# A selective-scan kernel: products with C of a turn as one GpSimd instruction, and the steps around them put into other turns

## The chip, the cores and the metric

The kernel runs on one core of a Trainium2 chip. The metric is the device time of one execution in microseconds (us). Five engines work side by side, each through its own queue in program order: PE (TensorE, matmuls), DVE (VectorE), ACT (ScalarE), POOL (GpSimd) and SP, which issues the DMAs here. An instruction starts when its engine is free and the semaphores that it waits for have been raised.

## The reference, cut to what matters

Eight images of 48x48 positions and 96 channels pass through four layers, each as `x = x + layer(group_norm(x))`. Layers 0 and 3 (called ss2d) and layer 2 (called `lines`) are selective scans; layer 1 is a spectral layer that the change does not touch. A scan layer does this for four directions over the image (rows, columns, and both backwards), with 192 inner channels d and 16 states s:

```python
xz = x @ in_w;  xc, z = split(xz)
u  = silu(conv(xc) + conv_b)            # 3x3 depthwise in ss2d, 4 taps along the line in `lines`
dt_low, B, C = split(u @ x_proj)        # 6 + 16 + 16 values at each position
dt = softplus(dt_low @ dt_w + dt_b)     # step size, one for each d and position
for each position l in order:           # for each d and each state s
    h = exp(dt[l] * A) * h + dt[l] * u[l] * B[l]
    y[l] = sum over s of h * C[l]
y  = y + D * u                          # then, over the directions, merged
```

In ss2d the merged result is normalised over d, multiplied by `silu(z)` and projected to 96 channels. In `lines` the state starts from zero in every line of 48, each direction is multiplied by `silu(z)` and projected, and added to x.

## The kernel before, in words

**Tiling.** A scan layer is a list of blocks: image ("job") by direction by row group of 10, 10, 10, 10 and 8 lines (480 or 384 columns): 160 blocks a layer. A block has 8 *slots* (two halves of 96 channels by four groups of states), a slot has 3 *units*, and a unit is a tile of 128 partitions by n columns (32 channels by 4 states; a few columns more in ss2d for the carried state). Two slots make a *turn*, so a block has four turns, q0 to q3, a layer 640 turns, the kernel 1920. The number of a slot over all blocks is t or `at`; slot 0 is the first of q0.

**A turn.** For turn t the following are written out, in this order (lines 382 to 403):

- DVE: `scan(t, 0)`, the products dbu = dt·u·B of the next turn's first slot, `scan(t, 1)`, those of the next turn's second slot, `scan(t, 2)`. One scan covers two units and runs in place over dbu (L296).
- ACT: the decay factors exp(dt·A), two units at a time into one of two PSUM buffers `ps_da` (`make_da`, L288), and a copy of B into the PSUM buffer `ps_b` (`copy_b`, L245), from which DVE reads it.
- POOL: the product h·C of the turn before's second slot (`make_hc(t-1, 1)`, L302), the units of dbu that DVE leaves over (`make_dbu`, L264), a preparation of the carried state (`begin`), and the product h·C of this turn's first slot. The table `ON_POOL` says how many of a slot's three units POOL makes: slots 1, 3 and 7 two, slot 5 three.
- PE: `reduce(t-1, 0)` and `reduce(t-1, 1)`, each 4 x 3 = 12 matmuls in tiles of the array (L322) and 4 more (L324), which sum h·C over states. They wait for the products.

**Beside the scans.** Twice in a turn `aside` is called, after `reduce(t-1, 1)` for the slot `at = 2t` and at the turn's end for `at + 1`. It loads B and C of the next block (`load_bc`) and its step sizes (`load_dd`) in the slots that `LOAD_BC` and `LOAD_DD` name, takes one step of the side work (`next(beside)`), runs the planned steps of slot `at`, and then what `later` and `tail` hold. All of these stand in the engines' queues at that place.

- The planned steps are `stage1` of a block to come: the projection to dt_low, B and C (ss2d: s0, L642; copied to `bcl` by ACT, L647), the step sizes (`raw`, L632; `biased`, L636; softplus, L660), their products with u on POOL (`make_du`, L449, one instruction for each half, two in a block), and the stores to DRAM (`store_dd`, L434), from which `load_dd` broadcasts them. `plan` places them two blocks ahead, at slots 0 to NG+2 with NG = 8. In `lines` the steps are the convolution (L771), its silu (L778), the projection (L788), the softplus (L806), the z gate (L812, L820) and the stores.
- The side work of ss2d for job j is `post` of job j-1 (norm and output projection, lines 527 to 586; its steps alternate PE, DVE and ACT and are a slot apart), the group norm of the next job, and from 10 x 8 = 80 used slots on the convolution of the next job (lines 500 to 525): eight slots for each half of a row group, with PE matmuls in six of them, a z matmul in the seventh, and two silu on ACT in the eighth. For the last job `post` runs two steps a slot, behind the row groups as they finish.
- In `lines` the end of a direction's block comes through `done`: DVE's product with the gate (L834), one slot later `project` on PE (L843), another slot later `add` on DVE (L849 or L851).

Softplus, silu and exp lie in different table sets of ACT; a change loads a table.

The buffers of B and C are six tiles (`NBUF`), the first `LEAD` columns of each zero; a tile holds B and then C of one group of states and serves two slots of a block.

Of the kernel before, what the change touches and what calls it, by code (L numbers as in the profile page):

```python
# [31 lines left out]
LOAD_BC = (2, 3, 6, 7)  # L32
LOAD_DD = (4, 5)
NBUF = 6
UP = 96
# [5 lines left out]
CH = 96  # L41
ON_POOL = {1: 2, 3: 2, 5: 3, 7: 2}

# [52 lines left out]
def vss_stack_kernel(ctx: ExitStack, tc: tile.TileContext, i: dict, out: bass.AP):  # L96
# [88 lines left out]

    def scans(dirs, order, restart, a, pools, ps, stage1, opening, done, side, tail):

# [16 lines left out]
        rooms = [pools["dbu"].tile([P, 6 * WMAX], F32, tag="dbu", name="dbu") for _ in range(NG // 2)]  # L204
        bufs = [pools["bc"].tile([P, LEAD + 2 * BMAX], F32, tag=f"bc{n}", name=f"bc{n}") for n in range(NBUF)]
        for buf in bufs:
            nc.gpsimd.memset(buf[:, :LEAD], 0.0)
        for room in rooms:
            nc.gpsimd.memset(room, 0.0)
        dbus, das, bps, bcs, ys = {}, {}, {}, {}, {}  # L210
        later, ends = {}, []
# [8 lines left out]
        def load_bc(t):  # L220

            b, slot = blocks[t // NG], t % NG
            sg = ORDER[slot][1]
            other = t - slot + NG - 1 - slot
            n = min(free, key=lambda n: free[n])
            free[n] = other
            r = bufs[n]
            rows4 = b.bcd[8 * sg:8 * sg + 8, :].rearrange("(s w) n -> s (w n)", w=2)
            nc.sync.dma_start(r[:, LEAD:LEAD + 2 * b.n], rows4.unsqueeze(0).to_broadcast([32, 4, 2 * b.n]))

            lo, hi = LEAD - b.at.start, LEAD + b.n
            bcs[t] = bcs[other] = r[:, lo:hi + b.at.start], r[:, hi:hi + b.n]

        def copy_b(t):

            if t >= NG * len(blocks):
                return
            b, slot = blocks[t // NG], t % NG
            if slot == NG // 2:
                bps[t] = bps[t - 1]  # L240
                return
            if ON_POOL.get(slot) == 3:
                return
            bps[t] = ps("b", 1)
            nc.scalar.copy(bps[t][:, :bcs[t][0].shape[1]], bcs[t][0])  # L245

        def units(tile, b, lo, hi):
            return tile[:, lo * b.m:hi * b.m].rearrange("p (u m) -> p u m", m=b.m)

        def make_dbu(t, engine):  # L250

            if t >= NG * len(blocks):
                return
            b, slot = blocks[t // NG], t % NG
            if t // 2 not in dbus:
                dbus[t // 2] = rooms[t // 2 % (NG // 2)]
            cut = 3 - ON_POOL.get(slot, 0)
            lo, hi = (0, cut) if engine is nc.vector else (cut, 3)
            if lo == hi:
                return  # L260
            o = units(dbus[t // 2], b, 3 * (slot % 2) + lo, 3 * (slot % 2) + hi)[:, :, b.by]
            du = b.got[ORDER[slot][0]][:, lo:hi, 1, b.by]
            by = (bps[t] if engine is nc.vector else bcs[t][0])[:, b.by]
            engine.tensor_mul(o, du, by.unsqueeze(1).to_broadcast([P, hi - lo, by.shape[1]]))  # L264
# [32 lines left out]

        def make_hc(t, sub):
            b, q = turns[t]
            n = b.n  # L300
            h = units(dbus[t], b, 3 * sub, 3 * sub + 3)[:, :, b.at]
            nc.gpsimd.tensor_mul(h, h, bcs.pop(2 * t + sub)[1].unsqueeze(1).to_broadcast([P, 3, n]))  # L302

# [37 lines left out]

        for n, b in enumerate(blocks[:2]):
            plan(b, NG * (n - 2))
        for t in range(-2 * NG, 0):
            run(t)
# [29 lines left out]
        for t, (b, q) in enumerate(turns):  # L375
            at, nblk = 2 * t, t // (NG // 2)
            if q == 0:
                if nblk + 2 < len(blocks):
                    plan(blocks[nblk + 2], at)
                if b.k == order[0] and b.first:  # L380
                    beside = side(b.job)
            scan(t, 0)
            if t > 0:
                make_hc(t - 1, 1)
            make_dbu(at + 2, nc.vector)
            make_da(t, 1)
            make_dbu(at + 3, nc.gpsimd)
            if t > 0:
# [8 lines left out]
            begin(t + 2)  # L397
            make_hc(t, 0)
            make_da(t + 1, 0)
# [4 lines left out]
            if q == NG // 2 - 1 and b.k == order[-1] and b.last:  # L404
                for _ in beside:
                    while tail:
                        tail.pop(0)()
        make_hc(nt - 1, 1)
        for sub in range(2):
# [33 lines left out]

    def make_du(b, half, u):


        n = b.n
        dt, du = sizes(b, half)
        nc.gpsimd.tensor_mul(rows(du, n), rows(dt, n), u)  # L449
        if b.m == b.n:  # L450
            at = SEG - 1 if b.rev else 0
            nc.gpsimd.memset(rows(dt, n)[:, :, at:at + 1], FAR)
        elif half == 0:

# [5 lines left out]
    def ss2d(l, xin, xout, b0=0):  # L460
# [3 lines left out]
        def pool(name, bufs, **kw):  # L464
            return stack.enter_context(tc.tile_pool(name=name, bufs=bufs, **kw))
        wt, big, zp, lnp, xio = pool("wt", 1), pool("big", 3), pool("z", 1), pool("ln", 2), pool("xio", 2)
        zdr = pool("zdr", 3, space=DRAM)
# [31 lines left out]

        def conv(b, blks):  # L500
            if blks[0] == BLKS[0]:
                us[b] = big.tile([DH, 2, L], F32, tag="big", name="u")
                zs[b] = zdr.tile([DH, 2, L], F32, tag="z", name="zd")
            for r0, nr in blks:
                n = nr * SEG
                for half in range(2):
                    pu = side_psum()
                    for slot in range(7):
# [6 lines left out]
                        if slot == 6:  # L515
                            pz = ps("s1", 1)
                            nc.tensor.matmul(pz[:DH, :n], lhsT=w[f"{l}_in"][:, (2 + half) * DH:(3 + half) * DH],
                                             rhs=xpad[:C, 1 + r0:1 + r0 + nr, 1:1 + W], start=True, stop=True)
                        yield
                    s = slice(r0 * W, r0 * W + n)  # L520
                    nc.scalar.activation(us[b][:, half, s], pu[:DH, :n], AF.Silu, bias=w[f"{l}_cb"][:, half:half + 1])
                    z = zp.tile([DH, BMAX], F32, tag="z", name="z")
                    nc.scalar.activation(z[:, :n], pz[:DH, :n], AF.Silu)
                    yield
# [63 lines left out]
        def side(job):  # L588
# [17 lines left out]
            if more:  # L606
                for _ in front(job + 1):
                    used += 1
                    yield
                while used < 10 * NG:  # L610
                    used += 1
                    yield
                yield from conv(job + 1, BLKS)
            else:
# [10 lines left out]
        def stage1(b):  # L625
# [35 lines left out]

            def du(half):
                return lambda: make_du(b, half, u[:, half])

            def store(half):
                return lambda: store_dd(b, half)

            return {0: s0, 1: s1, 3: s3, 4: s4, 5: lambda: biased(1), 6: s6, 7: du(0), 8: du(1),
                    NG + 1: store(0), NG + 2: store(1)}

# [14 lines left out]

        dirs = DIRS_SS
        load_x(0)
        for _ in front(0):
            pass
        for _ in conv(0, BLKS[:3]):  # L690
            pass
        scans(dirs, (0, 1, 3, 2), False, a, pools, ps, stage1, opening, done, side, [])
        for _ in post(nb - 1, BLKS[:1]):
# [4 lines left out]
    def lines(xin, xout):  # L698
# [56 lines left out]
        def stage1(b):  # L755
# [53 lines left out]
            def s7():  # L809
                for half in range(2):  # L810
                    got["z", half] = ps("s1", 2)
                    nc.tensor.matmul(got["z", half][:DH, :n], lhsT=w["l2_inz"][:, b.k, half * DH:(half + 1) * DH],  # L812
                                     rhs=shifted(0)[:C], start=True, stop=True)
                for half in range(2):
                    make_du(b, half, rows(b.ub[:, half], n))

            def s8():
                b.zb = up.tile([DH, 2, BMAX], F32, tag="zb", name="zb")
                for half in range(2):
# [49 lines left out]
        for _ in front(0):  # L869
            pass  # L870
        scans(dirs, range(NK), True, a, pools, ps, stage1, opening, done, side, tail)
        stack.close()
# [288 lines left out]
```

## Time and profile before

| | us |
|---|---|
| median of 3 runs | 18841.26 (18840.8 to 18842.25) |
| profiled execution | 18848.6, span 18846.8, mean granted TensorE clock 0.767 |
| layer 0 (ss2d) | about 119 to 5733 |
| layer 1 (spectral) | about 5800 to 7100 |
| layer 2 (`lines`) | about 7167 to 13077 |
| layer 3 (ss2d) | about 13204 to 18817 |

A block of ss2d takes 35.0 us on average, one of `lines` 37.0. The costliest instructions are the scans (L296, 5760 of them, 2.1 us each), the products with C (L302, 3840, 2.6 us each), the decay factors (L288, 11520, 0.65 us each) and the reductions.

A row of the group view reads: line, engine, operation, output<-inputs, shape and count, then busy time and mean ns of one, then the engine's idle time just before these instructions and what ended it. A row of the timeline reads: start, duration, engine, line, operation, and in brackets the idle time before it with its releaser. Runs of equal neighbours are one row there with a count. "PEld" is TensorE's weight load. A wait for several semaphores is put down to the one that came last.

### The profile page before, as it was taken

The page shows a single profiled execution, that of the slowest core. Times are in us where ns is not written, and L with a number is a line of the kernel's source. Part 1 is how long each engine was busy: PE and PEld are TensorE (multiplying, and loading weights), DVE is VectorE, ACT ScalarE, POOL GpSimd, SP SyncE. Part 2 cuts the span into 40 slices and gives each one's busy share as a digit, 9 for nine tenths or more (in the row PEclk, how much of TensorE's full clock was granted, in tenths as well). Part 3 has the DMA queues.
Part 4 walks back from the last instruction along what each step waited for, and adds up shares of the span by engine and source line. Part 5 has one row for each costly group of instructions (what it writes and reads, how often), then busy time and mean ns, then how long its engine had stood idle before and what let it go on. Part 6 is the DMA issues. An engine that isn't in the chain of part 4 may idle for free.

```text
span 18846.8 us, 169421 instructions
## 1 busy us (share of the span) xinstructions
PE 14864.5 (79%) x53500; PEld 4298.7 (23%) x53500; DVE 16139.5 (86%) x10809; ACT 13830.0 (73%) x20502; POOL 15203.6 (81%) x8316
## 2 busy tenths in 40 slices
PE   6777777777777897888988988888677777777776
PEld 1211211211214562222222222222121121121121
DVE  7999999999993227999999999997999999999998
ACT  6777777777772227888888888886778778778776
POOL 7899899899891007888888888886899999999998
PEclk7776776776767787888888888888777777677776
DMA  4545445445453334444444444443454554554444
GB/s 138 167 166 166 167 166 168 165 166 170 161 171 60 48 46 141 154 146 153 156 147 150 151 155 148 148 154 119 164 170 162 169 170 161 169 168 161 169 166 146
DMA packets 768461, 2836.57 MB, mean 151 GB/s; under 512 B 235724, under 2 KB 298668, under 8 KB 640926
## 3 DMA queue, kind: packets, MB, share of 16 engines
q1 hardware_dynamic: 767558, 2825.75, 45.5%
q8 instruction: 418, 6.85, 0.2%
q14 instruction: 485, 3.97, 0.1%
HBM read 2377.32 MB, written 448.17 MB: 150 GB/s over the span
## 4 chain that ended last, share of the span: by engine, by line
DVE 24%; PE 21%; ACT 18%; POOL 17%; issue 12%; DMA 7%; SPq 0%; POOLq 0%; DVEq 0%; ACTq 0%
DVE dbu L296 15%; POOL dbu L302 12%; DVE dbu L264 7%; ACT ps_da L288 5%; PE ps_s L771 4%; ACT L288 4%; POOL dbu L264 4%; DMA dd<-dd 3%; PE ps_y L322 3%; DMA dd<-dds 2%; PE ps_h L1001 2%; PE ps_y L1014 2%; POOL dds L449 1%; PE ps_side L512 1%; PE ps_s L642 1%
## 5 line engine op out<-in xcount | busy, mean ns | idle before, releaser
L296 DVE TENSOR_TENSOR_SCAN dbu<-ps_da,dbu 128x968 f32<-128x968 f32 (+3 forms) x5760 | 11853.6, 2076 | 1080.1 <-ACT ps_da L288 1002.8
L302 POOL TENSOR_TENSOR dbu<-dbu,bc 128x1440 f32<-128x1440 f32 (+1 forms) x3840 | 10060.1, 2634 | 1877.1 <-DVE dbu L296 1715.4
L288 ACT ACTIVATE ps_da<-dd,w_l_a 128x484 f32<-128x484 f32 (+3 forms) x11520 | 7440.1, 650 | 2865.8 <-DVE dbu L296 2652.9
L322 PE MATMUL ps_y<-dbu,w_red 128*32 128x480 f32 (+1 forms) x23040 | 4834.2, 736 | 2581.2 <-POOL dbu L302 2578.1
L324 PE MATMUL ps_y<-dbu,w_red 128*32 128x480 f32 (+1 forms) x7680 | 4795.5, 736 | 0.0
L264 DVE TENSOR_TENSOR dbu<-dd,ps_b 128x1443 f32<-128x1443 f32 (+7 forms) x3360 | 3895.9, 1159 | 292.9 <-ACT ps_b L245 217.5
L264 POOL TENSOR_TENSOR dbu<-dd,bc 128x962 f32<-128x962 f32 (+7 forms) x1920 | 3889.3, 2026 | 96.5 <-DMA dd<-dd 50.0
L322 PEld LDWEIGHTS ps_y<-dbu,w_red 128*32 128x32 f32 x23040 | 756.2, 125 | 6399.6 <-POOL dbu L302 4693.7
L771 PE MATMUL ps_s<-xpad,w_l_cw 128*128 128x480 f32 (+1 forms) x2560 | 1753.3, 837 | 2.6 <-ACT xpad L144 1.6
L245 ACT COPY ps_b<-bc 128x482 f32<-128x482 f32 (+3 forms) x2880 | 1543.4, 536 | 283.4 <-DVE dbu L264 257.3
L512 PE MATMUL ps_side<-xpad,w_l_cw 128*128 128x480 f32 (+1 forms) x2880 | 1613.8, 688 | 5.8 <-ACT xpad L144 4.5
L288 ACT ACT_TABLE_LOAD x986 | 1265.0, 1283 | 17.3
L133 POOL MEMSET w_l_cw<- 128x1760 f32 (+1 forms) x3 | 5.8, 1942 | 1344.4 <-DVE x L981 1339.0
L642 PE MATMUL ps_s<-u,w_l_xp 96*38 96x480 f32 (+1 forms) x1280 | 932.9, 868 | 2.8 <-ACT dds L636 1.5
L632 PE MATMUL ps_s<-bcl,dtw 6*96 6x480 f32 (+1 forms) x1280 | 830.1, 735 | 125.2 <-ACT dds L636 114.9
L449 POOL TENSOR_TENSOR dds<-dds,u 96x480 f32<-96x480 f32 (+1 forms) x640 | 765.8, 1196 | 182.9 <-ACT dds L660 182.8
L318 PE MATMUL ps_y<-ysum,w_ident 96*96 96x480 f32 (+1 forms) x960 | 754.3, 875 | 134.1 <-ACT ysum L683 133.2
L512 PEld LDWEIGHTS ps_side<-xpad,w_l_cw 128*128 128x128 f32 x2880 | 571.2, 223 | 1119.3 <-issue 922.3
L771 PEld LDWEIGHTS ps_s<-xpad,w_l_cw 128*128 128x128 f32 x2560 | 517.5, 207 | 1075.5 <-issue 976.0
L324 PEld LDWEIGHTS ps_y<-dbu,w_red 128*32 128x32 f32 x7680 | 693.7, 125 | 0.0
L788 PE MATMUL ps_s<-ub,w_l_xp 96*38 96x480 f32 (+1 forms) x640 | 376.8, 724 | 271.9 <-ACT ub L778 271.8
L812 PE MATMUL ps_s<-xpad,w_l_inz 96*96 96x480 f32 (+1 forms) x640 | 506.7, 926 | 79.7 <-ACT dds L806 60.2
(147 smaller groups left out, 11761.0 us busy)
## 6 DMA issues: line engine op xcount, KB each, us to landing
dd<-dd SPq DMA_DIRECT2D x512, 1452.0 KB
bc<-bcd SPq DMA_DIRECT2D x1536, 480.0 KB
dd<-dd SPq DMA_DIRECT2D x256, 1440.0 KB
dd<-dds SPq DMA_DIRECT2D x512, 363.0 KB
dd<-dd SPq DMA_DIRECT2D x128, 1164.0 KB
bc<-bcd SPq DMA_DIRECT2D x384, 384.0 KB
dd<-dds SPq DMA_DIRECT2D x256, 360.0 KB
dd<-dd SPq DMA_DIRECT2D x64, 1152.0 KB
```

What stands on the lines that cost most here:

```text
L245: nc.scalar.copy(bps[t][:, :bcs[t][0].shape[1]], bcs[t][0])
L264: engine.tensor_mul(o, du, by.unsqueeze(1).to_broadcast([P, hi - lo, by.shape[1]]))
L288: nc.scalar.activation(da[:, at:at + b.m], b.got[half][:, u % 3, 0, :], AF.Exp, scale=a[:, b.k, ci:ci + 1])
L296: nc.vector.tensor_tensor_scan(db, da, db, 0.0, ALU.mult, ALU.add)
L302: nc.gpsimd.tensor_mul(h, h, bcs.pop(2 * t + sub)[1].unsqueeze(1).to_broadcast([P, 3, n]))
L322: nc.tensor.matmul(y[32 * g:32 * g + 32, :n], lhsT=wc["red"][:, :32], rhs=hc[:, g, b.at], start=False, stop=(slot == 3))
L324: nc.tensor.matmul(y[DH:, :n], lhsT=wc["red"][:, 32:], rhs=hc[:, 2, b.at], start=(slot == 0), stop=(slot == 3))
L449: nc.gpsimd.tensor_mul(rows(du, n), rows(dt, n), u)
L512: nc.tensor.matmul(pu[:, :n], lhsT=flat[:, at:at + P], rhs=xpad[:, r0 + dy:r0 + dy + nr, dx:dx + W], start=(tap == 0), stop=(tap == 8))
L632: nc.tensor.matmul(got["p"][:DH, :n], lhsT=dtw[2 * NS:, b.k, half, :], rhs=b.bcl[2 * NS:, :n], start=True, stop=True)
L642: nc.tensor.matmul(got["p"][:NBC, :n], lhsT=w[f"{l}_xp"][:, b.k, half, :], rhs=u[:, half], start=(half == 0), stop=(half == 1))
L771: nc.tensor.matmul(got["u", half][:, :n], lhsT=flat[:, at:at + P], rhs=shifted(off), start=(tap == 0), stop=(tap == 3))
```

## The change

1. `make_hc(t)` multiplies all six units of a turn with C in one GpSimd instruction; it is issued after `scan(t+1, 0)`, for the turn that has just ended. So that C of two slots is one operand, the buffers of B and C become one tile with seven places, and the operand steps from one place to the other (backwards where needed).
2. `ON_POOL` becomes two tables, and POOL may make units of a turn's first slot too. ss2d: one unit of slots 2, 5 and 6, three of slots 3 and 7. `lines`: two of slot 3, three of slots 5 and 7, one of slot 6. Both still give nine units a block to POOL. Slot 4 takes over slot 3's copy of B only if there is one.
3. `make_du` multiplies both halves in one instruction; in ss2d it stands at slot 7 only (before at 7 and 8), and the stores at NG and NG+1 (before one later each).
4. In ss2d the projection s0 is at slot -1 (before 0), so blocks are planned three ahead. `load_dd` of the first half is at slot 3 (before 4), in all scan layers.
5. The convolution of the side work starts five slots sooner (after 75 used slots), which puts its silu into another turn; its z matmul goes into `tail`, behind the other steps of its slot.
6. Buffers: the block input in `post` has one instead of two, the gate `zb` in `lines` two instead of three.

The core of the diff:

```diff
-LOAD_DD = (4, 5)
-NBUF = 6
+LOAD_DD = (3, 5)
+NBUF = 7
-ON_POOL = {1: 2, 3: 2, 5: 3, 7: 2}
+ON_POOL_SS = {2: 1, 3: 3, 5: 1, 6: 1, 7: 3}
+ON_POOL_L2 = {3: 2, 5: 3, 6: 1, 7: 3}
...
-        bufs = [pools["bc"].tile([P, LEAD + 2 * BMAX], F32, tag=f"bc{n}", name=f"bc{n}") for n in range(NBUF)]
+        bufs = pools["bc"].tile([P, NBUF, 2 * LEAD + 2 * BMAX], F32, tag="bc", name="bc")
...
-        def make_hc(t, sub):
+        def make_hc(t):
             b, q = turns[t]
             n = b.n
-            h = units(dbus[t], b, 3 * sub, 3 * sub + 3)[:, :, b.at]
-            nc.gpsimd.tensor_mul(h, h, bcs.pop(2 * t + sub)[1].unsqueeze(1).to_broadcast([P, 3, n]))
+            h = dbus[t][:, :6 * b.m].rearrange("p (k u m) -> p k u m", k=2, m=b.m)[:, :, :, b.at]
+            at, to = cs.pop(2 * t), cs.pop(2 * t + 1)
+            bcs.pop(2 * t), bcs.pop(2 * t + 1)
+            end = to + (1 if to > at else -1)
+            c = bufs[:, at:(None if end < 0 else end):to - at, LEAD + n:LEAD + 2 * n]
+            nc.gpsimd.tensor_mul(h, h, c.unsqueeze(2).to_broadcast([P, 2, 3, n]))
...
             scan(t, 0)
             if t > 0:
-                make_hc(t - 1, 1)
+                make_hc(t - 1)
             make_dbu(at + 2, nc.vector)
             make_da(t, 1)
+            make_dbu(at + 2, nc.gpsimd)
             make_dbu(at + 3, nc.gpsimd)
...
             begin(t + 2)
-            make_hc(t, 0)
             make_da(t + 1, 0)
...
-    def make_du(b, half, u):
+    def make_du(b, u):
-        n = b.n
-        dt, du = sizes(b, half)
-        nc.gpsimd.tensor_mul(rows(du, n), rows(dt, n), u)
+        dt, du = [b.dds[:, :, n, b.at].rearrange("p h (r s) -> p h r s", s=SEG) for n in range(2)]
+        nc.gpsimd.tensor_mul(du, dt, u)
...
-                while used < 10 * NG:
+                while used < 10 * NG - 5:
                     used += 1
                     yield
-                yield from conv(job + 1, BLKS)
+                yield from conv(job + 1, BLKS, tail.append)
...
-            return {0: s0, 1: s1, 3: s3, 4: s4, 5: lambda: biased(1), 6: s6, 7: du(0), 8: du(1),
-                    NG + 1: store(0), NG + 2: store(1)}
+            return {-1: s0, 1: s1, 3: s3, 4: s4, 5: lambda: biased(1), 6: s6, 7: du,
+                    NG: store(0), NG + 1: store(1)}
```

## The prediction

> **What bounds the kernel now.** I read the page's busy table first. Its columns are busy time, share of the span and instructions.
>
> ```profile
> PE 14864.5 (79%) x53500; PEld 4298.7 (23%) x53500; DVE 16139.5 (86%) x10809; ACT 13830.0 (73%) x20502; POOL 15203.6 (81%) x8316
> DVE  7999999999993227999999999997999999999998
> PEclk7776776776767787888888888888777777677776
> ```
>
> VectorE leads in the three scan layers (slices of nines); the gap in the middle is the spectral layer, which the change does not touch. GpSimd's 81% and TensorE's 79% are near enough to become the bound locally. Then the costliest groups, for who waits on whom:
>
> ```profile
> L296 DVE TENSOR_TENSOR_SCAN dbu<-ps_da,dbu 128x968 f32<-128x968 f32 (+3 forms) x5760 | 11853.6, 2076 | 1080.1 <-ACT ps_da L288 1002.8
> L302 POOL TENSOR_TENSOR dbu<-dbu,bc 128x1440 f32<-128x1440 f32 (+1 forms) x3840 | 10060.1, 2634 | 1877.1 <-DVE dbu L296 1715.4
> L322 PEld LDWEIGHTS ps_y<-dbu,w_red 128*32 128x32 f32 x23040 | 756.2, 125 | 6399.6 <-POOL dbu L302 4693.7
> ```
>
> VectorE stands idle 1080 us ahead of its scans, 1003 of them for ScalarE's decay factors (ps_da): that is all a better order could win. GpSimd's products with C wait for the scan and TensorE waits for the products (4694 us), so GpSimd is not a bound by itself, but its product starts everything that TensorE does in a turn. The same group from 1000 to 5000 us (an ss2d layer; blocks of 35.0 us, 114 of them) and from 8000 to 12000 us (`lines`; 37.0 us, 108):
>
> ```profile
> L296 DVE TENSOR_TENSOR_SCAN dbu<-ps_da,dbu 128x968 f32<-128x968 f32 (+1 forms) x1368 | 2811.9, 2080 | 262.0 <-ACT ps_da L288 235.6 <-POOL dds L449 15.4 <-POOL dbu L302 6.6
> ```
> ```profile
> L296 DVE TENSOR_TENSOR_SCAN dbu<-ps_da,dbu 128x960 f32<-128x960 f32 (+1 forms) x1297 | 2672.2, 2067 | 252.3 <-ACT ps_da L288 252.0
> ```
>
> So 235.6/114 = 2.1 us a block in ss2d, 2.3 in `lines`. ScalarE's timeline in a convolution block names the causes: softplus and silu with their table loads of 1.28 us, between decay factors.
>
> ```profile
> 1406.78 1.28 ACT L660 ACT_TABLE_LOAD   x1
> 1408.07 1.01 ACT L660 ACTIVATE dds<-dds 96x960 f32<-96x960 f32 x1
> 1409.10 1.28 ACT L288 ACT_TABLE_LOAD   x1
> 1412.26 1.28 ACT L521 ACT_TABLE_LOAD   x1
> ```
>
> Last, a turn with post work, over all engines (start, duration):
>
> ```profile
> 2996.75 2.74 POOL L302 TENSOR_TENSOR dbu<-dbu,bc 128x1440 f32<-128x1440 f32 x1
> ...
> 2999.54 1.02 PE L322 MATMUL ps_y<-dbu,w_red 128*32 128x480 f32 x3 [2.06 <-POOL dbu L302]
> ...
> 3001.30 3.36 PE L548 MATMUL ps_side<-ones,sq 96*96 96x1 f32 x20
> ...
> 3002.64 2.16 DVE L296 TENSOR_TENSOR_SCAN dbu<-ps_da,dbu 128x968 f32<-128x968 f32 x1
> ...
> 3004.73 0.13 DVE L551 COPY var<-ps_side 96x5 f32<-96x5 f32 x1
> ```
>
> The product ends at 2999.5, the reductions follow, then the variance matmuls, and VectorE's copy of their result starts at 3004.73, as they end (3004.66) and as the last scan ends (3004.80). The slack of this handoff from TensorE to VectorE is zero. That place decides my forecast.
>
> **The change, part by part.**
>
> The merged product. L302 costs 2736 ns at 1440 elements and 2227 at 1152 (rows of the ss2d layer): 1.77 ns an element and 0.19 us an instruction. One of 2880 is 0.19+2880×1.77 = 5.29 us against 5.47 for two: 0.19×1920 turns = 357 us of GpSimd. It is not on the path, so I count nothing for it. The operand with C is now strided over the seven buffers. The nearest row for a strided operand is L449, 1.03 us in rows and 1.45 in column views, so 2.63 ns an element, 7.8 us a product; the other end is 5.1, with no fixed cost left. I take 5.3, as the inner rows of C stay contiguous, unlike the column views.
>
> What moves with it: before, slot 0's product ran inside the turn and only slot 1's (2.74) came after the turn's last scan. Now both come after it, and both reductions (four groups of four; starts 0.43 us apart at full clock, at 9028.94 us, and 0.80 at half, at 2999.54) wait for it. TensorE's side work in a turn starts 5.3−2.7 = 2.6 us later, plus 0.8 to 1.6 for the reductions that could be done early before. Behind the waiting matmul in TensorE's queue stand the side matmuls; for them wait VectorE (post, add), ScalarE (raw, silu), and GpSimd (du).
>
> Units of B by turn. On VectorE L264 costs 1632 ns for three units, 630 for one, so about 1130 for two. Per ss2d block before 4×1632+3×630 = 8418, after 3×1632+3×1130 = 8286; `lines` after 4×1632+630+1130 = 8288. That is −0.13 us × 480 = −62 us, contained in the sums below. GpSimd's nine units a block stay (1.05, 1.89 and 2.74 us for one to three). The turn with slots 2 and 3 gets 5.3+1.05+2.74 = 9.1 us of GpSimd in about 9. `lines` loses one copy of B (0.55 us, ScalarE, hidden). Turns change length: VectorE's turn q3 gets 1.05 longer, q0 and q2 shorter.
>
> Step products as one: 1.03×2 against about 1.9 (L575, 960 elements, 1.88). It runs behind softplus and ahead of the next product in GpSimd's queue; the store of half 0 then waits 1 us more. SP's queue is passed by: a load at slot 3 ahead of that store, so later loads of B and C start 4 to 5 us later, needed more than a turn after; counted at 0. The single buffer of the block input makes a load wait for the store before it, four slots (17 us) ahead of its use: 0 too. The z gate's matmul goes behind the other steps of its slot, ahead of its silu still: 0. If these covers are gone, the dearest row is 0.35 us a block (37.3 us of DMA waits in 108 blocks of `lines`), 170 us.
>
> Projection a slot sooner, silu of the convolution in turn q1 instead of q3's end. Of ss2d's 35.7-us convolution blocks 32.8 are VectorE's work, 2.9 stalls. After: 32.7 work; ScalarE in q1 has six decay factors 4.0, copies 1.1, silu with tables 3.8 = 8.9 against a turn of 8.8, so 0.6 to 0.8 late in q2; the chain in q2's end, product 5.3, reductions 1.6, two taps 1.85, raw 1.05, biased 0.65, decay pair 1.37 = 11.8 against 10.9, 0.4 to 1.0 at full clock and 2.0 to 2.6 at half; softplus ahead of the next q0, 1.2. Sum 35.0 to 35.4, or 36.7 to 37.1: −0.7 to +1.4. I take +0.3, as the granted clock lies between (0.71 by the window below): ×140 blocks = **+42 us**.
>
> Post blocks. Ten handoffs of a job (14 jobs) lie within one turn. TensorE is 3.4 to 4.2 us later, VectorE 1.05 earlier in q0 and q2 and later in q1 and q3, and of that part was slack: about 1.2 us stall at full clock, 4.3 at half. 140 handoffs give 168 to 602 us, midway 385; while VectorE waits there, ScalarE gets ahead, which saves up to 2.1 us in each of 88 blocks, 185. That leaves 200; I take 2.5 us a block, 220, with +50 and +600 as ends: **+220 us**.
>
> The clock in question (columns: length, busy time and count of PE, PEld, DVE, ACT, POOL, then granted clock, DMA share, GB/s):
>
> ```profile
> 2996.00:3005.00 9.00, 6.94 (x37) 3.68 (x30) 8.86 (x7) 6.51 (x11) 8.94 (x8) 0.50 0.36 90
> 3011.00:3018.00 7.00, 5.45 (x30) 1.12 (x22) 6.70 (x5) 4.14 (x7) 6.57 (x3) 0.99 0.80 297
> 3000.00:4000.00 1000.00, 760.59 (x2736) 194.91 (x2728) 933.15 (x615) 762.16 (x1150) 911.05 (x513) 0.71 0.50 166
> ```
>
> A reduction takes double in the first stretch. [...]
>
> Other ss2d blocks (320−140−88 = 92) lose a third of their 2.1-us stalls, as softplus now falls into the 9.3-us turn: −0.7×92 = **−65 us**. The last job's post, two steps a slot: **+30**.
>
> `lines`. At q0 the silu stall is 1.57 us a block; the longer q3 takes away 1.4 of it. In q1 the add waits for TensorE:
>
> ```profile
> 9025.00 1.03 POOL L449 TENSOR_TENSOR dds<-dds,ub 96x480 f32<-96x480 f32 x1
> ...
> 9026.16 2.73 POOL L302 TENSOR_TENSOR dbu<-dbu,bc 128x1440 f32<-128x1440 f32 x1
> ...
> 9030.52 1.85 PE L843 MATMUL ps_s<-gated,wo 96*96 96x480 f32 x4 [0.57 <-ACT zb L820]
> ...
> 9032.77 0.62 DVE L851 TENSOR_TENSOR x<-x,ps_s 96x480 f32<-96x480 f32 x1
> ```
>
> The product there ends 2.6 us later, then both reductions (1.6, or 3.2) and L843: 0.9 us of stall at full clock, 2.4 to 4 at half. Row blocks −0.7 to +1.2, taken +0.6×80 = **+48**; column blocks, whose TensorE is idle only 2 to 4 us a block, 0 to +2.3, taken +1.0×80 = **+80**.
>
> Sum: 42+220−65+30+48+80 = +355 us. The profiled execution took 18848.6 us (span 18846.8), 0.04% above the median of 18841.3, so 19,204; I say **19,200**.
>
> **The rivals.**
> 1. Faster, by the stalls. If TensorE's results still come before VectorE asks, the handoffs cost nothing, and silu and softplus, now in turns apart and longer, no longer delay decay factors: half of 1002.8 goes. 18848.6−501 = 18,350. For it: ScalarE's decay factors (L288) wait 2653 us for scans, so it has room; against it: the zero slack at 3004.73. It decides if a handoff stalls under 0.3 us. With TensorE at full clock throughout, in between (handoffs at 0, convolution −0.7×140, others −65, rows −0.7×80): 18,630.
> 2. No change: handoffs cost 220 and the other blocks give it back; 18,840.
> 3. The strided product is dear. GpSimd has 3×1.05+2×2.74+2 = 10.6 us beside four products in 35, so from 6.1 us a product it is the bound; at 7.8 a block takes 42 us: 480×7 = +3400, 22,200. Against it: contiguous inner rows.
>
> **How the numbers follow.** Forecast 0.58, rival 1 0.32 (0.20 at 18,350, 0.12 at 18,630), rival 2 0.06, rival 3 0.04. Upper ends of all terms: 1.4×140+600−0+60+1.2×80+2.3×80 = +1136, which needs all at once; I stop at 19,720 (+870). Low end 18,330, just under rival 1. The forecast's own range is 18,900 to 19,720. A change of 0.2% is about what can be told from none: faster 0.32, same 0.06, slower 0.62.
>
> **What would show it.** Right: products with C near 5.3 us, 1920 of them; idle of L540, L551, L584, L851 for PE in the hundreds of us; clock below 0.767. Wrong: those idle times stay near what they are and idle ahead of L296 for ps_da falls towards 500 us (rival 1); L302 above 6 us and VectorE under 80% busy (rival 3). What would make me wrong most likely is the lateness of TensorE, worked out for one turn and applied to 140 handoffs.

## The result, and the profile after

The changed kernel takes 19,786.9 us (median of 4 runs, 19,766.7 to 19,802.7) against 18,841.8 in the same comparison: 1.0500 times as long, with a 95% interval of 1.0482 to 1.0519. It is 945 us slower. The forecast was slower by 355 us, with 19,720 as the upper end; the direction was right, the size was not, and the time lies outside the range. The profiled execution took 19,766.7 us (span 19,765.0), 918 us of span more than before.

The same lines of the page and the same groups as before, now of the changed kernel. Its line numbers are other: L298 is the scan, L309 the merged product, L329 the reduction.

```profile
PE 14657.8 (74%) x53500; PEld 4423.6 (22%) x53500; DVE 16207.1 (82%) x10329; ACT 13682.4 (69%) x20342; POOL 14882.1 (75%) x6061
DVE  6889889888883227888888888886888888888888
PEclk7777777777767778888888888887777777777776
...
L298 DVE TENSOR_TENSOR_SCAN dbu<-ps_da,dbu 128x968 f32<-128x968 f32 (+3 forms) x5760 | 11823.6, 2075 | 1286.5 <-ACT ps_da L290 1099.0
L309 POOL TENSOR_TENSOR dbu<-dbu,bc 128x2880 f32<-128x2880 f32 (+1 forms) x1920 | 9760.3, 5083 | 2067.3 <-DVE dbu L298 1978.5
...
L329 PEld LDWEIGHTS ps_y<-dbu,w_red 128*32 128x32 f32 x23040 | 973.1, 139 | 8037.0 <-POOL dbu L309 5904.6
```

GpSimd is busy 321 us less (357 were worked out for the product), and every other engine is busy for a smaller share. No engine became the bound; all wait more for each other. TensorE's weight loads wait 5905 us for the product (4694 before). VectorE's waits of the changed kernel (line that waits, for whom: us in total, times, longest) show where the time arrived:

```profile
DVE dbu L298 <- ACT ps_da L290: 1099.0, 872, 4.9
DVE x L861 <- PE ps_s L853: 242.4, 119, 3.5
DVE gated L844 <- PE ps_y L331: 170.5, 137, 9.0
DVE xi L594 <- PE ps_side L591: 163.3, 38, 6.6
DVE var L561 <- PE ps_side L558: 131.0, 44, 3.4
DVE x L859 <- PE ps_s L853: 66.6, 40, 3.4
```

Before, the same waits were 1003, 33, 33, 52, 9 and 33 us; the second of them in the view of before:

```profile
DVE x L851 <- PE ps_s L843: 33.4, 34, 2.8
```

The handoffs from TensorE grew as the prediction has it, but the wait for decay factors, which rival 1 had falling by half, grew too. In this table each layer is measured from its first scan's start to its last scan's end in the profiled execution; the runs under it are the experiments below.

| run | median us | ss2d | lines | ss2d |
|---|---|---|---|---|
| before | 18,842 | 5614 | 5910 | 5612 |
| after | 19,787 | 5928 | 6197 | 5931 |
| two products, old places (e1) | 18,777 | 5456 | 6173 | 5453 |
| merged product alone (e2) | 19,782 | 5938 | 6206 | 5940 |
| two products, both late (e3) | 18,920 | 5559 | 6099 | 5556 |
| after + zero-weight matmuls (e4) | 19,239 | 5658 | 6217 | 5661 |
| after + biased later (e5) | 19,357 | 5716 | 6213 | 5719 |
| after + post spaced (e6) | 19,811 | 5952 | 6190 | 5948 |
| before + zero-weight matmuls (e7) | 18,973 | 5684 | 5914 | 5674 |
| e4 and e5, and zero weights in rows of lines (e8) | 19,366 | 5655 | 6339 | 5658 |
| after, lines' loads as before (e9) | 19,708 | 5934 | 6125 | 5930 |
| e1, lines' loads as before (b1) | 18,558 | 5449 | 5954 | 5449 |
| b1 + zero weights, two du in lines (b2) | 18,761 | 5595 | 5882 | 5600 |
| b1 + two du in lines (b3) | 18,485 | 5454 | 5877 | 5454 |

### The profile page after: what moved, and what is told of

It reads as the page before. It is cut to its first block, busy times and chain, and to the rows that moved or that the text cites. A ratio compares the mean times of both kernels' runs of the same rounds, so it can differ in the third digit from the quotient of the medians.

```text
span 19765.0 us, 165309 instructions
## 1 busy us (share of the span) xinstructions
PE 14657.8 (74%) x53500; PEld 4423.6 (22%) x53500; DVE 16207.1 (82%) x10329; ACT 13682.4 (69%) x20342; POOL 14882.1 (75%) x6061
## 4 chain that ended last, share of the span: by engine, by line
PE 29%; POOL 22%; ACT 18%; DVE 16%; issue 8%; DMA 6%; SPq 0%; POOLq 0%; DVEq 0%; ACTq 0%
POOL dbu L309 17%; DVE dbu L298 11%; PE ps_y L329 11%; ACT ps_da L290 7%; PE ps_s L782 4%; DVE dbu L266 4%; POOL dds L455 3%; DMA bc<-bcd 3%; PE ps_side L518 3%; DMA dd<-dds 2%; PE ps_h L1011 2%; ACT L671 2%; PE ps_y L1024 1%; ACT L290 1%; PE ps_s L643 1%
## 5 line engine op out<-in xcount | busy, mean ns | idle before, releaser
L298 DVE TENSOR_TENSOR_SCAN dbu<-ps_da,dbu 128x968 f32<-128x968 f32 (+3 forms) x5760 | 11823.6, 2075 | 1286.5 <-ACT ps_da L290 1099.0
L309 POOL TENSOR_TENSOR dbu<-dbu,bc 128x2880 f32<-128x2880 f32 (+1 forms) x1920 | 9760.3, 5083 | 2067.3 <-DVE dbu L298 1978.5
L329 PE MATMUL ps_y<-dbu,w_red 128*32 128x480 f32 (+1 forms) x23040 | 5180.3, 814 | 4247.1 <-POOL dbu L309 4206.7
L331 PE MATMUL ps_y<-dbu,w_red 128*32 128x480 f32 (+1 forms) x7680 | 5154.5, 814 | 0.0
L266 DVE TENSOR_TENSOR dbu<-dd,ps_b 128x962 f32<-128x962 f32 (+5 forms) x2880 | 3830.6, 1330 | 309.0 <-ACT ps_b L247 259.9
L266 POOL TENSOR_TENSOR dbu<-dd,bc 128x481 f32<-128x481 f32 (+5 forms) x2240 | 3912.3, 1761 | 43.1 <-DMA bc<-bcd 38.4
L329 PEld LDWEIGHTS ps_y<-dbu,w_red 128*32 128x32 f32 x23040 | 973.1, 139 | 8037.0 <-POOL dbu L309 5904.6
L247 ACT COPY ps_b<-bc 128x482 f32<-128x482 f32 (+3 forms) x2720 | 1444.9, 531 | 235.7 <-DMA bc<-bcd 168.5
L455 POOL TENSOR_TENSOR dds<-dds,u 96x960 f32<-96x960 f32 (+1 forms) x320 | 706.0, 2206 | 1050.6 <-ACT dds L671 1050.6
L694 ACT COPY ysum<-ps_y 96x480 f32<-96x480 f32 (+1 forms) x640 | 475.4, 743 | 729.6 <-PE ps_y L331 729.6
L331 PEld LDWEIGHTS ps_y<-dbu,w_red 128*32 128x32 f32 x7680 | 893.3, 139 | 0.0
L653 PE MATMUL ps_s<-u,w_l_xp 96*38 96x480 f32 (+1 forms) x1280 | 838.0, 785 | 16.8 <-ACT z L533 13.8
L643 PE MATMUL ps_s<-bcl,dtw 6*96 6x480 f32 (+1 forms) x1280 | 767.3, 683 | 34.3 <-ACT dds L647 29.3
L647 ACT ACTIVATE dds<-ps_s,w_l_dtb 96x480 f32<-96x480 f32 (+1 forms) x640 | 405.5, 634 | 520.4 <-PE ps_s L643 490.0
```

What stands on the lines that cost most here:

```text
L247: nc.scalar.copy(bps[t][:, :bcs[t].shape[1]], bcs[t])
L298: nc.vector.tensor_tensor_scan(db, da, db, 0.0, ALU.mult, ALU.add)
L309: nc.gpsimd.tensor_mul(h, h, c.unsqueeze(2).to_broadcast([P, 2, 3, n]))
L329: nc.tensor.matmul(y[32 * g:32 * g + 32, :n], lhsT=wc["red"][:, :32], rhs=hc[:, g, b.at], start=False, stop=(slot == 3))
L331: nc.tensor.matmul(y[DH:, :n], lhsT=wc["red"][:, 32:], rhs=hc[:, 2, b.at], start=(slot == 0), stop=(slot == 3))
L455: nc.gpsimd.tensor_mul(du, dt, u)
```

## The experiments

The theory to be tested was the prediction's: TensorE's work of a turn starts late behind the merged product, and what waits for it stalls. The rival: the moved steps (silu, softplus, lengths of turns) cost the time.

**Which part.** In e1 the changed kernel gets its two products back, at their old places; in e2 the kernel before gets the merged product alone (with the one tile of seven buffers, and one buffer less for the block input and for the gate; plan, s0, du, the stores and the convolution's start are as before, left out below).

```diff
 e1, against after:
-                make_hc(t - 1)
+                make_hc(t - 1, 1)
...
             begin(t + 2)
+            make_hc(t, 0)
 e2, against after:
+LOAD_DD = (4, 5)
...
+ON_POOL_SS = {1: 2, 3: 2, 5: 3, 7: 2}
+ON_POOL_L2 = {1: 2, 3: 2, 5: 3, 7: 2}
...
```

> The changed kernel with the product with C as two instructions again, at their old places (slot 0's inside the turn, slot 1's after the next turn's first scan); units of B, du, projection, convolution and buffers stay as changed. Theory 'late TensorE' (TensorE's work of a turn starts 2.6 us later behind the merged product, and what waits for it stalls: 247 us more in post, 381 us in lines, and the 1.3 us a block that the trace of after newly shows ahead of q3's second scan, some 300 us): most of the 945 us comes back, 18,800 to 19,000 us. Rival 'moved steps' (silu, softplus and the turns' new lengths cost it, the product only stands beside them): 19,400 to 19,800 us.

> The kernel before with the merged product alone (one tile of seven buffers for B and C with it, and one buffer less of the block input and of the gate); units of B, du, projection, loads and convolution as before. 'Late TensorE': post +250, lines +380, raw and silu chains some more, 19,400 to 19,700 us. 'Moved steps': 18,800 to 18,950 us.

Measured: e1 18,776.7 us, 0.9963 [0.9949, 0.9978] of before; e2 19,781.6, 1.0499 [1.0483, 1.0515]. The product alone costs 939 us, as much as the whole change and 80 us more than the range expected for e2 allows. Taking it out of the change brings 1010 back, a little more than expected. The rival falls as the cause of the slowdown. But the moved steps aren't neutral: beside two products they gain 158 us in each ss2d layer (5614 to 5456) and lose 263 in `lines`; more on that below.

**One product or two in the same place.** In e3 both products stand after the next turn's first scan, one behind the other.

```diff
...
-                make_hc(t - 1)
+                make_hc(t - 1, 0)
+                make_hc(t - 1, 1)
...
```

> The changed kernel with the product as two instructions, both after the next turn's first scan, one behind the other. The first half's reductions may start 2.6 us sooner than with the merged product, the second half's 0.2 us later. If the end of the last product sets the stalls and the clock doesn't matter: 19,780 to 19,950 us. If the work that is gathered behind one wait (both reductions, at half clock after the gap) matters: 19,200 to 19,600 us.

Measured: 18,919.6 us, 1.0041 [1.0026, 1.0056] of before. 867 of the 945 us are gone, more than either theory expected. But the last product does not end 0.2 us later, as the expectation had it. A product of three units need not wait for the turn's last scan: in 689 of the 1278 turns of ss2d that have a next turn in their layer, the first one starts before that scan ends, the merged one in none. Counted from the end of that scan, on average over these turns, the first reduction starts after 3.25 us instead of 6.04, and the last product ends after 5.20 instead of 5.93. So what the merging takes away is the early first half; how much of the 867 us comes from the earlier start of the reductions, and how much from the earlier end, e3 doesn't separate. In the trace the reductions also run faster: a reduction matmul of 480 columns takes 0.60 us at full clock and 1.02 at half (in after, at a granted clock of 1.00 from 1477.4 to 1485 us and of 0.50 from 1470.3 to 1474), and in the first layer the share above 0.75 us, which the counts below take as half clock, is 0.49 before, 0.68 after, 0.49 in e1 and 0.51 in e3.

**The chain.** A convolution block of the changed kernel around q3's second scan (the rows of the chain; rows between them are left out):

```profile
1465.02 5.29 POOL L309 TENSOR_TENSOR dbu<-dbu,bc 128x2880 f32<-128x2880 f32 x1 [2.46 <-DVE dbu L298]
1470.37 1.02 PE L329 MATMUL ps_y<-dbu,w_red 128*32 128x480 f32 x3 [5.09 <-POOL dbu L309]
1471.17 1.02 PE L329 MATMUL ps_y<-dbu,w_red 128*32 128x480 f32 x3
1471.97 1.02 PE L329 MATMUL ps_y<-dbu,w_red 128*32 128x480 f32 x3
1472.77 1.02 PE L329 MATMUL ps_y<-dbu,w_red 128*32 128x480 f32 x3
1473.72 2.67 PE L518 MATMUL ps_side<-xpad,w_l_cw 128*128 128x480 f32 x4
1476.33 1.04 PE L643 MATMUL ps_s<-bcl,dtw 6*96 6x480 f32 x2
1477.40 0.66 ACT L647 ACTIVATE dds<-ps_s,w_l_dtb 96x480 f32<-96x480 f32 x1 [2.99 <-PE ps_s L643]
1477.96 2.64 ACT L290 ACTIVATE ps_da<-dd,w_l_a 128x484 f32<-128x484 f32 x4
1479.42 2.17 DVE L298 TENSOR_TENSOR_SCAN dbu<-ps_da,dbu 128x968 f32<-128x968 f32 x1 [3.04 <-ACT ps_da L290]
```

Read from the end: VectorE waits 3.04 us for decay factors, ScalarE stands 2.99 us at biased(1) (L647) for raw(1) on TensorE (L643), that stands behind two taps, these behind four groups of reductions 0.80 us apart, and these 5.09 us behind the product. (The four groups are both reductions of a turn together: 23040 records of L329 and 7680 of L331 in 1920 turns are 12 and 4 a turn. The description of the kernel ahead has 12 and 4 for each reduction, twice as many.) ScalarE has nothing to do but stands in front of its own queue. e5 puts biased(1) one slot later, behind those decay factors.

```diff
             def s6():
+                biased(1)
                 both = b.dds[:, :, 0, b.at]
                 nc.scalar.activation(both, both, AF.Softplus)
...
-            return {-1: s0, 1: s1, 3: s3, 4: s4, 5: lambda: biased(1), 6: s6, 7: du,
+            return {-1: s0, 1: s1, 3: s3, 4: s4, 6: s6, 7: du,
```

> The changed kernel with ss2d's biased(1) on ScalarE one slot later, ahead of softplus, so that q3's second pair of decay factors no longer stands behind it in ScalarE's queue. If the 1.3 us a block ahead of q3's second scan is the chain product, reductions, taps, raw, biased: that stall goes and some of it shows up again at q0 behind softplus; 19,400 to 19,600 us. If it is ScalarE's own load in that turn: 19,730 to 19,850 us.

Measured: 19,356.9 us, 430 less than after, a little more than the chain was expected to give. The stall ahead of q3's second scan falls from 1.84 to under 0.05 us a block in the 140 blocks with convolution, and VectorE's whole wait for decay factors from 1099 to 717 us. Softplus, 0.65 us later, does not bring it back at q0 (1.10 to 1.13).

**The clock.** e4 gives TensorE something to do while it waits: in ss2d, ahead of a turn's reductions, matmuls with zero weights into the sums.

```diff
+            if sub == 0 and not restart:
+                for _ in range(4):
+                    for g in range(3):
+                        nc.tensor.matmul(y[32 * g:32 * g + 32, :n].rearrange("p (a c) -> p a c", c=32), lhsT=wc["red"][:, 32:],
+                                         rhs=wc["red"][:, :32].unsqueeze(1).to_broadcast([P, n // 32, 32]), start=False, stop=False)
```

> The changed kernel, and in ss2d, ahead of a turn's reductions, four groups of three matmuls with zero weights, which add nothing to the sums and stand in TensorE's queue while it waits for the merged product (the layer lines is left alone). Theory 'half clock behind the wait' (in ss2d 0.69 of the reduction matmuls ran at half clock, against 0.50 before): the share falls below 0.4, the reductions end up to 1.6 us sooner, and the two ss2d layers lose 100 us or more each of their 5930 us; 19,400 to 19,600 us. Rival 'only the lateness': the share may fall, but the time doesn't, and the extra matmuls delay the side work: 19,780 to 20,000 us.

Measured: 19,238.8 us, 548 less than after, with more work, and below the range that the theory expected. The two ss2d layers lose 270 us each; `lines`, left alone, stays (6217). The reductions above 0.75 us fall to 0.02. The same block as above, now in e4, rows left out as there:

```profile
1414.42 5.30 POOL L309 TENSOR_TENSOR dbu<-dbu,bc 128x2880 f32<-128x2880 f32 x1 [2.46 <-DVE dbu L298]
1414.89 3.42 PE L330 MATMUL ps_y<-w_red 128*32 128x480 f32 x24
1419.77 0.60 PE L334 MATMUL ps_y<-dbu,w_red 128*32 128x480 f32 x3 [1.46 <-POOL dbu L309]
1421.52 1.88 PE L523 MATMUL ps_side<-xpad,w_l_cw 128*128 128x480 f32 x4
1424.40 0.66 ACT L652 ACTIVATE dds<-ps_s,w_l_dtb 96x480 f32<-96x480 f32 x1 [1.93 <-PE ps_s L648]
1426.42 2.17 DVE L298 TENSOR_TENSOR_SCAN dbu<-ps_da,dbu 128x968 f32<-128x968 f32 x1 [0.64 <-ACT ps_da L290]
```

L330 are the added matmuls, two records for each of the twelve. The taps start 1.75 us after the first reduction instead of 3.35 and take 0.8 less, and of the 3.04-us stall 0.64 is left. Over all turns of ss2d the reductions as a whole gain less than the theory had: counted as above, the first starts 0.40 us later than in after (6.44 instead of 6.04) and the last ends 0.35 earlier (8.51 instead of 8.86). The side matmuls behind them gain as well: a tap takes 580 ns on average instead of 677 (1000 to 5000 us). Windows over the first ss2d layer, of after and of e4 (length, PE, PEld, DVE, ACT, POOL, granted clock, DMA share, GB/s):

```profile
118.00:6046.00 5928.00, 4112.66 (x15196) 1113.44 (x15200) 5241.05 (x3174) 4305.59 (x6487) 4989.87 (x2203) 0.74 0.45 156
```
```profile
119.00:5777.00 5658.00, 5233.48 (x30514) 1561.95 (x30515) 5236.44 (x3174) 4301.19 (x6486) 4991.66 (x2204) 0.98 0.48 164
```

TensorE is busy 1121 us more and the layer is 270 us shorter. The reductions behind the 5.09-us wait at 1470.37 run at half clock (1.02 us), those behind 1.46 us at 1419.77 at full (0.60). Over the ss2d layers of after, the first reduction of a turn ran at half in all 565 turns in which TensorE had stood idle for 3 us or more just before it, in 171 of the 213 with 2 to 3 us, and in 32 of the 304 with less than 1 us. The trace of before is less clear (106 of 138 turns with 3 us or more, and 347 of 891 with less than 1), so the wait just before a matmul is not all that counts there.

The same matmuls in the kernel before, as a control (the same diff):

> The kernel before with the same zero-weight matmuls in ss2d ahead of a turn's reductions (in the changed kernel they took 270 us off each ss2d layer). If the half clock behind a wait costs only where the merged product makes TensorE's work late: ss2d stays within 30 us of its 5613 us a layer, the whole 18,790 to 18,900. If it costs before too (half of its reduction matmuls run at half clock): 100 us or more off each layer, below 18,640.

Measured: 18,973.4 us, 1.0075 [1.0058, 1.0092] of before: the layers got 70 and 62 us longer, outside both expectations. The share at half clock fell from 0.49 to 0.01, and it did not help. Before, the chain was not the last to arrive: the stall ahead of q3's second scan in the convolution blocks was 0.00 us a block, and with the added matmuls it became 0.33, so there they seem only in the way.

e8 puts e4 and e5 together, and zero-weight matmuls into the row directions of `lines` too.

> The changed kernel with both edits that helped ss2d alone (biased(1) at slot 6: -215 us a layer; zero-weight matmuls: -270), and the zero-weight matmuls in the row directions of lines too. If both take away the same stall ahead of q3's second scan: ss2d 5560 to 5640 us a layer, so about -300 to -370 each; if they add up, 5450. In lines, if half clock makes half of the add's 2.0 us stall, the two row directions lose about 1 us a block of their 37.9 and 39.6, -80 us. Whole 18,950 to 19,150 us.

Measured: 19,365.5 us. In ss2d 5655 and 5658 us, no better than e4 alone: the two gains don't add up. In the convolution blocks the stall ahead of q3's second scan is gone (0.32 us a block in e4), but the one ahead of q1's rose from 0.55 to 1.09; why is not shown. In `lines` it failed: 6339 us, 142 more. There VectorE's wait for the sums (gated) rose from 170 to 372 us, so the extra matmuls seem to have delayed what they should have sped up. How much of the loss in `lines` is clock is left open.

**The handoffs of post.** In e6 the first loop of post gets a slot more, so that no handoff falls inside a turn; the group norm behind it waits two slots instead of seven (`rest`), so that the convolution stays where it is.

```diff
-            yield from group_norm(x, lambda r0, nr: xpad[:C, 1 + r0:1 + r0 + nr, 1:1 + W], side_psum)
+            yield from group_norm(x, lambda r0, nr: xpad[:C, 1 + r0:1 + r0 + nr, 1:1 + W], side_psum, rest=2)
...
                 nc.scalar.activation(sq[:, :, :n], yc, AF.Square)
                 yield
+                if len(blks) == len(BLKS):
+                    yield
```

> The changed kernel with one slot more between square and variance in post's first loop, so that its five handoffs from TensorE to VectorE in one turn fall on turn boundaries (and five of the seven waiting slots of ss2d's group norm left out, so that the convolution stays where it is). If the handoffs stall for lateness within the turn: the 187 us ahead of VectorE's L550 and L561 fall under 50, 19,590 to 19,690 us. If the stall only moves to the next step: 19,760 to 19,810 us.

Measured: 19,811.0 us, 24 (0.1%) more than after, which is no gain. The wait of L561, 131 us, fell to 6, and L550's went from 56 to 44; but xi's add in the second loop waited 211 instead of 163, the scans 1181 instead of 1099, and the group norm 27 for TensorE. By blocks, the 84 post blocks got 43 us shorter, and the 36 blocks behind them (7 to 9 of a job), which hold the end of the longer post and the shortened group norm, 117 longer. The edit gave nothing back as a whole; whether spacing without a shorter group norm would is not shown. A wait listed against a line is not the price of that line.

**Why `lines` lost beside two products.** In e1, ScalarE's copies of B in `lines` (8 to 12 ms) wait for a DMA, and SP's queue stands before the load of the step sizes. First the ScalarE group, then SP's wait, both of e1:

```profile
L247 ACT COPY ps_b<-bc 128x480 f32<-128x480 f32 (+1 forms) x518 | 277.1, 535 | 295.3 <-DMA bc<-bcd 263.0 <-DVE dbu L266 20.0 <-DVE dbu L298 11.7
```
```profile
SPq L218 <- DMA dd<-dds: 1944.7, 205, 11.3
```

SP waited 1276 us there before the change. `LOAD_DD = (3, 5)` puts that load right after the store that it reads, which in `lines` is still at slot 2, and the loads of B and C stand behind it in the queue. b1 is e1 with slots 4 and 5 in `lines`; e9 is the changed kernel with them.

```diff
-LOAD_DD = (3, 5)
+LOAD_DD_SS, LOAD_DD_L2 = (3, 5), (4, 5)
...
-                if slot in LOAD_DD:
-                    load_dd(blocks[nblk], LOAD_DD.index(slot))
+                if slot in (LOAD_DD_L2 if restart else LOAD_DD_SS):
+                    load_dd(blocks[nblk], (LOAD_DD_L2 if restart else LOAD_DD_SS).index(slot))
```

> The kernel with two products at their old places and all the other changes (18,777 us), with the loads of the step sizes in lines at slots 4 and 5 again, as before; ss2d keeps slot 3. In that run lines took 6173 us, 263 more than before, and ScalarE's copies of B waited 263 us in 4 ms for the DMA of B and C, while SP's queue stood before the load of the step sizes for their store. If that load at slot 3 blocks the loads behind it: lines comes back to 5880 to 5950 us, the whole to 18,480 to 18,560. If it is the single du (store of half 0 an instruction later) or the new table: 18,700 to 18,790 us.

> The changed kernel with the loads of the step sizes in lines at slots 4 and 5 again. With the loads at slot 3, lines took 6197 us with the merged product and 6173 with two, as if the product cost nothing there. If the blocked loads of B and C hid it (two stalls, of which only the later one shows): lines stays at 6150 to 6200 with the merged product, against 5954 with two, so the product costs 200 to 250 us there; whole 19,740 to 19,790. If the product costs nothing in lines: 5950 to 6000, whole 19,540 to 19,590.

Measured: b1 18,558.4 us, 0.9849 [0.9835, 0.9864] of before, with `lines` at 5954; e9 19,707.5, with `lines` at 6125. So the load costs 219 us beside two products and 72 beside the merged one, and the merged product costs 24 beside the early load and 171 beside the late one (in e2, with all else in its old place, 296): neither of e9's expectations was hit, the two costs hide each other in part.

**A version that beats both.** b1 left 226 us of waits for the load of the step sizes. b2 makes du in `lines` two instructions again, so that the first store starts sooner, and tries the zero-weight matmuls in ss2d; b3 is without these.

> The 18,558-us kernel (two products at their old places, the other changes kept, loads of lines at slots 4 and 5) with the product of step sizes in lines as two instructions again, and the zero-weight matmuls in ss2d. In lines VectorE waited 226 us for the load of the step sizes (1.4 us a block in q3, 0.4 before). If the single du delays the first store: lines loses 100 to 160 of its 5954 us; if not, it stays. In ss2d about 1 us of stalls a block is left: 0 to 60 us a layer. Whole 18,330 to 18,480 us.

> The 18,558-us kernel (two products, loads of lines at slots 4 and 5) with the product of step sizes in lines as two instructions, and no zero-weight matmuls. They cost 145 us in each ss2d layer in the last run, where lines took 5882 us. ss2d back at 5449 us a layer, lines at 5870 to 5900: 18,470 to 18,510 us.

Measured: b2 18,760.5 us: `lines` 72 us shorter, but ss2d 146 and 151 longer, so the matmuls cost there too, twice what they do in e7. b3 18,485.4 us, 0.9806 [0.9788, 0.9823] of before: 360 us faster than before and 1302 faster than after. Its page and wait line:

```profile
PE 14845.4 (80%) x53500; PEld 4308.2 (23%) x53500; DVE 16123.6 (87%) x10329; ACT 13663.4 (74%) x20342; POOL 15180.6 (82%) x8301
```
```profile
DVE dbu L298 <- ACT ps_da L290: 426.2, 543, 3.4
```

The wait for decay factors falls from 1003 to 426 us. This is rival 1's gain, which the moved steps do bring once the product is out of the way.

## Why the prediction was wrong, point by point

Term by term, in us of the profiled executions:

| term of the sum | forecast | measured |
|---|---|---|
| convolution blocks (140) | +42 | +245 |
| post blocks (forecast 88; measured 84, the last job's post is counted below) | +220 | +153 |
| other ss2d blocks | −65 | +144 |
| last job | +30 | +92 |
| `lines` | +48 and +80 | +287 |
| sum | +355 | +921 (span +918) |

- *The merged product takes 5.3 us, not on the path.* The duration was right (5.29 us by the timeline; no strided penalty, so rival 3 is out). Its saving was worth nothing, as said.
- *TensorE's side work starts 2.6 us later, plus 0.8 to 1.6.* The lateness was right: on average over ss2d the last reduction of a turn ends 8.86 us after the turn's last scan instead of 5.40, 3.5 us later where 3.4 to 4.2 were worked out, and e2 shows that the merged product is the whole loss. What the lateness costs was wrong, in the terms below. Behind the wait the four groups run at half clock more often (0.68 instead of 0.49), and the prediction took values between the two ends, near the full-clock one in post. e4, which brings the full clock back (0.98 granted over the first layer instead of 0.74), takes 270 us off each ss2d layer, net of what its own matmuls cost there, out of the 472 and 478 that separate after from e1.
- *Post blocks +220.* The 84 blocks measured got 153 us longer (3036 to 3189), and all waits of post's VectorE lines for TensorE grew by 247 (107 to 354). The term was somewhat too large, and the half-clock end, 600, did not come. e6's way of spacing the handoffs didn't give it back.
- *Convolution blocks +42.* The 140 blocks got 245 us longer (34.8 to 36.6 a block on average; the median block, the prediction's 35.7, went to 37.3). The chain was costed about right in its steps, with 2.0 to 2.6 of stall at half clock, and then averaged with the full-clock case by the mean granted clock: that averaging mis-sized the term, as the median block's +1.6 lies just above the half-clock end of +1.4, not at the +0.3 taken. The block shown above stalled 3.04. (The terms listed there add up to 34.9 to 35.7 and 36.5 to 37.3, not to the ends that the prediction gives; this changes little.)
- *Other ss2d blocks −65, last job +30.* This is the step that failed outright: the remaining blocks got 236 us longer (first job's first half 53, blocks 7 to 9 of a job 91, last job 92). The prediction charged the chain product, reductions, raw, biased, decay factors to the convolution blocks alone. But raw and biased are planned steps of every ss2d block, and so is the stall: ahead of q3's second scan 1.74 us a block in the first job's first half (0.12 before), 1.19 in blocks 7 to 9 and 0.95 in the last job (0.00 before). The gain booked for softplus was there (q0's stall 0.71 to 0.58 in the last job, 0.91 to 0.24 in blocks 7 to 9) and smaller than what came.
- *Lines +48 and +80.* The layer got 287 us longer. The add's wait grew by 243 us, twice the 128 of the term, and the gate product's by 138, which the prediction did not have; the silu stall at q0 gave 0.75 us a block back (1.49 to 0.74). Most of the gate product's wait is not the merged product's doing: it is 165 us in e1, with two products, and 59 in e2 (33 before). 72 of the 287 us are the early load's (e9). How the rest splits is not shown.
- *SP's queue, counted at 0, with 170 if the cover is gone.* The cover was gone in `lines`: 219 us beside two products, 72 beside the merged one. The prediction passed the load by in ss2d, where the stores also move a slot forward, and did not ask what the same constant does in `lines`, where they stay.
- *Rival 1, half of the stalls go.* The changed kernel didn't show it, but it is what the moved steps do without the merged product (499 of 1003 us are left in e1, 426 in b3). The time of rival 1, 18,350, was not reached by this alone: e1 took 18,777, and 18,558 with the loads of `lines` in their old place (b1). Gain and loss were both in the change: the product's loss alone is 939 us (e2), where all my terms made 355 in sum.
- *A clock below 0.767.* It rose to 0.775. The mean granted clock is over all time, the wait included (in the block shown above 0.83 from 1465 to 1470.3 us, in the wait, and 0.50 from 1470.3 to 1474, behind it); what goes with the longer chain is the clock in the first microseconds after the wait (share of reductions at half clock 0.49 to 0.68).

## What to carry to other kernels

Two short instructions that each wait only for their own inputs and each release part of a consumer's work can be worth far more than one that saves 0.2 us (867 us here, in e3): ask when the consumer gets its first piece, what it does meanwhile, and at which clock it then starts (1.02 us a reduction behind the long wait shown, 0.60 behind the short one of e4). Follow a late result through every queue that it stands in, in every kind of block, since an engine with time to spare still stops behind one waiting instruction (ScalarE, 69% busy, stood 2.99 us at biased(1)). A load that is moved toward its store can hold up all that stands behind it in its queue (219 us in `lines` beside two products); check it in each layer that shares the constant.

## What I had not expected of the hardware

Zero-weight matmuls in an otherwise idle wait made a layer 270 us shorter, although TensorE was busy 1121 us more; the mean granted clock of the run rose from 0.775 to 0.910. The same matmuls made the layer 62 to 70 us longer in the kernel before and about 150 longer in b2, two kernels in which VectorE hardly waits behind that chain without them (ahead of q3's second scan 0.00 us a block in the convolution blocks before, 0.08 in b1). Reductions that run in turns q0 and q2 of ss2d, behind the wait for one 5.3-us product, were at half clock in 0.88 of the cases, against 0.69 and 0.53 before; cutting that product in two at the same place in the queue brought them to 0.54 and 0.57 and took 867 us off.
